# Moving one more destination block from the counted path to the gathered path in a two-layer graph network

## The chip, the core and the metric

The kernel runs on one core of a Trainium2 chip. The metric is device time in microseconds (us), the median over runs of the same program on the same inputs. The core has five engines with instruction queues of their own: PE (TensorE, matrix products, with its weight loads listed apart as PEld), DVE (VectorE), ACT (ScalarE), POOL (GpSimd) and SP (SyncE, which here only issues transfers). SBUF is the on-chip memory, PSUM holds the sums of PE.

## The reference, cut to what matters

There are 6250 nodes with 128 features, and 200,000 edges sorted by destination, each with a source node, a destination node and 128 features of its own. The destination is `6250 * u**2` of a uniform `u`, so low nodes have many edges and high nodes few.

```
h = relu(layernorm(x))
agg_src  = segment_sum(h[src], dst);  agg_edge = segment_sum(edge_attr, dst)
x = x + relu(concat(h, agg_src, agg_edge) @ W.T + b)
h = relu(layernorm(x))
twice:  h = relu(segment_sum(h[src], dst) / max(deg, 1) @ W_l + b + h @ W_r)
x = x + h
```

So three times a sum over edges of gathered rows is needed (called layers 0, 1 and 2 below), and once a sum of the edges' own features.

## The kernel before, in words

Nodes are cut into NB = 49 blocks of 128. Edges are cut into tiles of 128 and groups of 1024 (U = 8 tiles); there are 196 groups. The sum over edges of `h[src]` into one destination block can be had in two ways, and the kernel uses both.

**Counted blocks.** For the first NC = 40 destination blocks the kernel builds, once, a matrix of counts: how many edges go from each source node to each destination node. Then the sum over edges into a destination block is a matrix product of the counts with the rows of all 49 source blocks, and this is done anew in each of the three layers.

**Gathered (listed) blocks.** The last NT = 9 destination blocks have few edges. Their source rows are fetched in every layer by an indirect transfer, 128 rows at a time, and summed by a product with a one-hot matrix of destinations. `LISTS` gives, for each such block, its first edge tile and the tile after its last. Neighbouring blocks share the tile in which their border lies.

The program has two stages.

*Stage 1 (to about 590 us): counting and edge sums.* A loop over the stretches (runs of one to fourteen groups) and, in them, over the GC = 177 groups whose edges reach counted blocks. For a counted group DVE makes two one-hot matrices (`sp`, `sq`, line 533), weighs one of them (L543) and, for late groups, a correction `sc` (L533 again). PE multiplies them tile by tile (L740 and, for the correction, L751) into the PSUM tile `pu`, and ACT copies each tile's window into a ring in SBUF (L766). When a stretch is finished, POOL writes its ring to the DRAM matrix `counts_d` (L793). Between these products the sums of edge features are threaded in (`sum_edges`): for all 196 groups, counted or not, SP loads the edge features (L618), DVE makes a one-hot (L620), PE multiplies (L629) and DVE adds into `aggE` (L635). `shares` spreads these 1568 tiles evenly over the counted groups. The first layer's normalised rows are made in passing, one block in every third group (`first_layer`). The last group of the counted part has a stretch of its own with a narrower ring (`ENDS`, 152 and 82 columns for the last two stretches). After stretch `EARLY - 1` the counts of the first block are loaded ahead of time (L642, on POOL's queue).

*Stage 2 (from about 590 us): three layers of block sums.* `neighbours(i)` runs once for each of 3 x 40 = 120 pairs of layer and counted block. It has 49 dense products on PE (L929, one per source block), each 128x128 by 128x256 (the rows are split in a high and a low part). The counts come from DRAM in loads of 1088 KB (L642, SP), in bytes, and six "pieces" per block are widened to 32 bits by ACT or DVE (L861, and a short one at L864). After the block's sum come a reduction (L954), the layer's own arithmetic, a transpose (L475) and a product with the next layer's weights (L482), and the rows are written to `rows_d` and `r_d` (L488, L489).

Work for the gathered blocks is woven into the dense products at fixed places (`at_step`, an event before dense product `s`). Their tiles are cut into batches of at most three (BT = 3); before the change there are 149 tiles in 51 batches. `gather` issues one indirect transfer per tile on POOL (L1016) into one of ROWS = 4 buffers `rows_t`. `prepare` copies and splits the rows (L1033 on ACT, L1040 on DVE), makes the one-hot (L1034, DVE) and then asks for the gather four batches ahead. `sum_rows` has one product per tile and block (L1062, PE, 161 per layer). `prepare` stands LEAD = 38 dense products ahead of its `sum_rows`. The batches are spread evenly over the layer by

```python
begin = 4 * NB + NB // 2 if layer == 0 else 4 * NB
end = (NC - 2) * NB + 24 if layer < 2 else (NC - 1) * NB + 16
s = begin + (end - begin) * m // (len(batches) - 1)
```

which is one batch per 33 to 35 dense products. PE's order in stage 2 is tied by explicit dependencies ("in its turn among the dense products"); on ACT and DVE the same helpers tie the preparations behind what the dense products need, and a scheduler places the rest by its own estimate of times.

The kernel checks on the chip that its constants suit the edges (the tile ranges of `LISTS`, the windows, the ring widths); if they did not, a slow general version would compute everything again.

Of the kernel before, what the change touches and what calls it, by code (L numbers as in the profile page):

```python
# [32 lines left out]
NK = 2  # L33
NC3 = 3
PIECES = (("pair", 0, 4, 1), ("pair", 4, 8, 0), ("pair", 8, 12, 1), ("pair", 12, 17, 1), ("third", 0, 4, 0), ("third", 4, 8, 1))
GC = 177
GT = 176
LISTS = (
    (1414, 1433), (1432, 1451), (1449, 1468), (1466, 1484), (1483, 1501), (1499, 1518), (1517, 1535), (1533, 1550), (1549, 1563),
)  # L40
LATER = (1, 0, 0, 1, 0, 1)
FIRST = (1, 1, 1, 1, 0, 1)
# [39 lines left out]
ENDS = (152, 82)  # L82
# [4 lines left out]
def kernel(ctx: ExitStack, tc: tile.TileContext, x, srcl, dstl, edge, w0t, b0, w1l, b1, w1r, w2l, b2, w2r, out):  # L87
# [25 lines left out]
    NC = NB - NT  # L113
    NX = (G - GT) // 2
    assert 2 * NX == G - GT and U * NX <= P
    live_in_last = U - unused // P
    NE = sum(t1 - t0 for t0, t1 in LISTS)
    NL = (2 * NX - 1) * U + live_in_last
    assert LISTS[-1][1] == GT * U + NL and LISTS[0][0] >= GT * U
    CU = GC * U  # L120
    win_of = lambda g: REGIONS[min(g // RUN, NR - 1)][4]
    regions = []
    for i, reg in enumerate(REGIONS):
        if i * RUN < GC:
            regions.append((i * RUN, min((i + 1) * RUN, GC) if i + 1 < NR else GC) + reg)
    SWMAX = max(r[5] for r in regions)
    stretches = []
# [4 lines left out]
    place_of = lambda g: sum(U // n for n in size_of[:g])  # L132
    places = place_of(GC)
    g, ng, *reg = stretches.pop()
    stretches += [(g, ng - 1, *reg[:3], ENDS[0], reg[4]), (g + ng - 1, 1, *reg[:3], ENDS[1], reg[4])]
    NS = len(stretches)
    EARLY = NS - 6
    batches, tiles = [], list(range(LISTS[0][0], LISTS[-1][1]))
    while tiles:
# [6 lines left out]
        marks = sorted((j, u) for u, (_, m) in enumerate(batch) for j in m)  # L146
        batches.append((batch[0][0] - GT * U, len(batch), marks))
    assert sum(len(marks) for _, _, marks in batches) == NE
# [28 lines left out]

    fast = ExitStack()
    const = fast.enter_context(tc.tile_pool(name="const", bufs=1))
    small = fast.enter_context(tc.tile_pool(name="small", bufs=4))  # L180
    work = fast.enter_context(tc.tile_pool(name="work", bufs=2))
    keep = fast.enter_context(tc.tile_pool(name="keep", bufs=1))

# [21 lines left out]
    lists = build.enter_context(tc.tile_pool(name="lists", bufs=1))  # L205
    p_e = lists.tile([P, GC, U, 2], F16, name="p_e")
    q_e = lists.tile([P, GC, U, 2], F16, name="q_e")
    w_e = lists.tile([P, GC, U, 2], I16, name="w_e")
# [363 lines left out]
    def list_load(h, s):  # L572


        for k, a in enumerate((srcl, dstl)):
            at_s = bass.AP(
                tensor=a.tensor, offset=a.offset + P // U * s * GU + (GT + h * NX) * U, ap=[[U, NX], [GU, P // U], [1, U]]
            )
# [939 lines left out]
```

## Time and profile before

| | us |
|---|---|
| median of 9 runs | 1525.94 (1521.47 to 1533.72) |
| the profiled execution's own time | 1516.44 |
| its span, first to last instruction | 1514.8 |
| stage 1, first dense product starts at | 589.9 |
| stage 2, last dense product starts at | 1508.4 |

The profiled execution is 1.64 us longer than its span, and 9.5 us shorter than the median. In the profile's rows "busy" is the time in which at least one such instruction runs; matrix products overlap each other, so a row's mean duration is longer than the distance from one product to the next. The idle time in a row is that of its engine just before such an instruction, and the name behind the arrow is what ended it.

### The profile page before, as it was taken

The numbers are of one execution on the slowest core, as the hardware profiler recorded it, in microseconds if no ns is written. First come the engines' busy times: TensorE is split into PE (matmuls) and PEld (weight loads), VectorE is DVE, ScalarE is ACT, GpSimd is POOL, SyncE is SP. The second block draws the span as 40 slices with busy tenths as digits, with TensorE's granted clock in tenths as the row PEclk, the third lists the DMA queues.
The fourth block names the chain that finished last, engine by engine and source line by source line (L and its number), as shares of the span: only waits on it lengthen the run. The fifth ranks groups of instructions, "written<-read, shape, count | busy, mean of one in ns | idle before, by whom it ended". The sixth has DMA issues, their size and how long they took to land.

```text
span 1514.8 us, 37416 instructions
## 1 busy us (share of the span) xinstructions
PE 1422.1 (94%) x12433; PEld 1380.6 (91%) x12433; DVE 1161.8 (77%) x3007; ACT 924.4 (61%) x2251; POOL 684.0 (45%) x921
## 2 busy tenths in 40 slices
PE   5899999999999999999999997999899999999998
PEld 4899999998999998999899997999889998988997
DVE  9897989888898999677677775667766766666674
ACT  2434444567777778676666675666656675655563
POOL 4435576400000001666565604775666236666661
PEclk9999999999999999999999999999999998999999
DMA  2789888998999998877767765766666666776672
GB/s 72 236 275 288 281 302 307 327 314 309 315 317 339 343 358 313 275 234 230 228 209 233 233 215 194 247 227 199 201 200 213 209 220 194 242 222 212 219 249 76
DMA packets 173764, 374.02 MB, mean 247 GB/s; under 512 B 29451, under 2 KB 118985, under 8 KB 154234
## 3 DMA queue, kind: packets, MB, share of 16 engines
q1 hardware_dynamic: 121454, 268.72, 53.4%
q0 software_dynamic: 22336, 88.52, 17.3%
q10 hardware_dynamic: 29772, 14.31, 3.3%
q8 instruction: 100, 1.64, 0.4%
q14 instruction: 102, 0.84, 0.2%
HBM read 289.32 MB, written 82.13 MB: 245 GB/s over the span
## 4 chain that ended last, share of the span: by engine, by line
PE 70%; DVE 7%; issue 7%; ACT 6%; POOL 4%; DMA 3%; ACTq 1%; another core or an unknown queue 1%; SPq 0%; DVEq 0%; POOLq 0%
PE ps L929 36%; PE pe L629 20%; POOL rows_t L1016 4%; PE pu L740 4%; PE ps_t L1062 3%; ACT ring L766 3%; PE pz L482 3%; PE pu L482 1%; DMA rows_t<-rows_d,row_i 1%; ACT wide L861 1%; DMA x_c<-in_x 1%; PE pz L475 1%; ACTq L526 1%; DVE terms L877 1%
## 5 line engine op out<-in xcount | busy, mean ns | idle before, releaser
L929 PE MATMUL ps<-terms,wide 128*128 128x256 f32 (+1 forms) x5760 | 812.3, 292 | 14.4 <-issue 11.5
L929 PEld LDWEIGHTS ps<-terms,wide 128*128 128x128 f32 x5760 | 754.0, 199 | 24.0 <-issue 15.8
L1016 POOL DMA_INDIRECT rows_t<-rows_d,row_i x447 | 498.4, 1115 | 378.4 <-issue 112.6
L629 PE MATMUL pe<-hot,edge_t 128*128 128x128 f32 x3136 | 473.2, 287 | 2.9 <-DVE aggE L635 1.8
L629 PEld LDWEIGHTS pe<-hot,edge_t 128*128 128x128 f32 x3136 | 395.3, 192 | 6.5 <-DVE aggE L635 2.7
L861 ACT CAST wide<-c 128x1024 fp32r<-128x1024 uint8 x239 | 284.6, 1208 | 125.5 <-PE ps L929 76.8
L766 ACT CAST ring<-pu 128x170 f32 (+5 forms) x736 | 205.0, 281 | 85.2 <-PE pu L751 46.2
L861 DVE CAST wide<-c 128x1024 fp32r<-128x1024 uint8 x241 | 174.5, 727 | 104.3 <-PE ps L929 82.5
L861 ACT CAST wide<-c_early 128x1024 fp32r<-128x1024 uint8 x118 | 140.4, 1204 | 69.0 <-PE ps L929 53.2
L740 PE MATMUL pu<-sq,sp 128*128 128x102 bf16 (+7 forms) x1416 | 170.9, 219 | 9.7 <-DVE sq L543 4.3
L793 POOL DMA_DIRECT2D counts_d<-ring x50 | 27.2, 543 | 287.4 <-ACT ring L766 171.8
L773 POOL TENSOR_TENSOR ring<-ring,fore 128x17 int32 x280 | 112.8, 403 | 87.7 <-ACT fore L761 34.9
L740 PEld LDWEIGHTS <-sp 128*128 128x128 bf16 x1416 | 118.9, 98 | 12.3 <-issue 5.8
L861 DVE CAST wide<-c_early 128x1024 fp32r<-128x1024 uint8 x122 | 88.0, 722 | 53.7 <-PE ps L929 41.4
L533 DVE TENSOR_TENSOR sq<-iota,q_e 128x816 bf16<-128x816 f16 (+7 forms) x177 | 123.2, 696 | 4.7 <-PE pu L751 4.1
L533 DVE TENSOR_TENSOR sp<-iota,p_e 128x1024 bf16<-128x1024 f16 x177 | 121.8, 688 | 3.6 <-PE pu L740 2.7
L1040 DVE TENSOR_TENSOR tw<-rows_t,tw 128x384 fp32r<-128x384 f32 x153 | 83.2, 544 | 39.2 <-ACT tw L1033 35.7
L751 PE MATMUL pu<-sc,sp 128*128 128x17 bf16 x745 | 95.8, 172 | 0.0
L620 DVE TENSOR_TENSOR hot<-iota,rel 128x64 f32<-128x64 f16 (+13 forms) x196 | 94.6, 483 | 0.0
L1062 PE MATMUL ps_t<-tw,hot_t 128*128 128x256 f32 (+1 forms) x483 | 85.8, 286 | 3.5 <-issue 2.7
L1034 DVE TENSOR_TENSOR hot_t<-iota_p,slot_e 128x384 fp32r<-128x384 f16 (+1 forms) x153 | 87.2, 570 | 0.0
L482 PE MATMUL pz<-w_sb,hT 128*128 128x256 f32 x196 | 62.8, 403 | 25.8 <-ACT hT L477 18.3
(195 smaller groups left out, 1412.0 us busy)
## 6 DMA issues: line engine op xcount, KB each, us to landing
edge_t<-in_edge SPq DMA_DIRECT2D x196, 512.0 KB
c<-counts_d SPq DMA_DIRECT2D x80, 1088.0 KB
c_early<-counts_d SPq DMA_DIRECT2D x39, 1088.0 KB
rows_d<-feats ACTq DMA_DIRECT2D x147, 64.0 KB
r_d<-r SPq DMA_DIRECT2D x147, 64.0 KB
own<-r_d SPq DMA_DIRECT2D x147, 64.0 KB
counts_d<-ring POOLq DMA_DIRECT2D x5, 1462.0 KB
rows_t<-rows_d,row_i POOLq DMA_INDIRECT x447
```

The costliest lines, as they stand in the source:

```text
L482: mm = nc.tensor.matmul(pz, hT, w_sb[layer], start=True, stop=True)
L533: nc.vector.tensor_tensor(to.rearrange("p t (c two) -> p t c two", two=2), iota[:, :m].rearrange("p (c two) -> p c two", two=2).unsqueeze( ...
L620: nc.vector.tensor_tensor(hot[:, : U * win].rearrange("p (u w) -> p u w", w=win), iota[:, :win].unsqueeze(1).to_broadcast([P, U, win]), re ...
L629: mm = nc.tensor.matmul(ps[:, :P], e[:, u, :], hot[:, u * win : u * win + P], start=u == 0, stop=u == U - 1)
L740: mm = nc.tensor.matmul(pu[:, i * HALF : i * HALF + nq], sp[:, t, :], sq[:, t, :nq], start=t == t0, stop=t == t0 + n - 1 and n > 1,)
L751: mm = nc.tensor.matmul(pu[:, i * HALF : i * HALF + NJ], sp_b[:, t, :], sc[:, slot + 1 - len(last_tiles) + j0, :NJ], start=False, stop=j0 ...
L766: put = nc.scalar.copy(ring[:, bass.ds(to_put[(g - g0) * U + t0], nq)], pu[:, i * HALF : i * HALF + nq])
L773: add = nc.gpsimd.tensor_tensor(to, to, fore[:, i, :], op=ALU.add)
L861: copied = copy(t[:, : p1 - p0], two)
L929: dense = nc.tensor.matmul(ps[:, :m], counts, terms_of(s, s + 1)[:, 0, :m], start=s == 0, stop=s == NB - 1)
L1016: it = nc.gpsimd.indirect_dma_start(out=rows[:, u, :], out_offset=None, in_=rows_d[layer][:, :], in_offset=bass.IndirectOffsetOnAxis(ap=ro ...
L1062: mm = nc.tensor.matmul(ps[:, :width], hot[:, k, :], tw[:, u, :width], start=begins, stop=ends)
```

## The change

One more destination block, block 39, is taken from the counted path and put on the gathered one. NT goes from 9 to 10 and NC from 40 to 39. The counted groups end two earlier (GC 177 to 175), and the list of sources begins two groups earlier (GT 176 to 174). The new list covers tiles 1397 to 1414, 18 tiles, of which tile 1414 is shared with the next block. The last stretch of the counted groups now has one group only, so it is not split any more and the stretches are 50 instead of 51. One pool of small tiles has three buffers of each instead of four.

```diff
-GC = 177
-GT = 176
+GC = 175
+GT = 174
 LISTS = (
-    (1414, 1433), (1432, 1451), (1449, 1468), (1466, 1484), (1483, 1501), (1499, 1518), (1517, 1535), (1533, 1550), (1549, 1563),
+    (1397, 1415), (1414, 1433), (1432, 1451), (1449, 1468), (1466, 1484), (1483, 1501), (1499, 1518), (1517, 1535), (1533, 1550), (1549, 1563),
 )
...
     g, ng, *reg = stretches.pop()
-    stretches += [(g, ng - 1, *reg[:3], ENDS[0], reg[4]), (g + ng - 1, 1, *reg[:3], ENDS[1], reg[4])]
+    if ng > 1:
+        stretches.append((g, ng - 1, *reg[:3], ENDS[0], reg[4]))
+    stretches.append((g + ng - 1, 1, *reg[:3], ENDS[1], reg[4]))
...
-    small = fast.enter_context(tc.tile_pool(name="small", bufs=4))
+    small = fast.enter_context(tc.tile_pool(name="small", bufs=3))
```

Counted over the whole program, the instructions change as follows.

| engine | fewer | more |
|---|---|---|
| PE | 147 dense products (L929), 16 counts (L740), 16 corrections (L751) | 54 products of gathered rows (L1062) |
| DVE | 9 widenings (L861), 3 short ones (L864), 2 each of `sp`, `sq`, weighing and `sc` (L533, L543) | 18 one-hots (L1034), 18 splits (L1040) |
| ACT | 9 widenings (L861), 16 ring copies (L766) | 18 copies of gathered rows (L1033) |
| POOL | 1 write of a ring (L793) | 51 indirect transfers (L1016) |
| SP | 3 loads of counts (L642) | none |

The reductions, transposes and products with weights (L954, L475, L482) keep their number, since every block still passes through them, on one path or the other. The batches per layer go from 51 to 57, and the dense products from one batch to the next from 33.3, 33.8 and 34.6 (layers 0, 1, 2) to 28.9, 29.3 and 30.0.

## The prediction

> **What bounds the kernel now.** I read the page's busy lines and slices first, then the windows by stage, then the chain, then PE's own timeline for prices.
>
> ```profile
> PE   5899999999999999999999997999899999999998
> ...
> POOL 4435576400000001666565604775666236666661
> ```
>
> PE is at nine tenths or more nearly throughout. POOL is idle late in stage 1 and about 60% busy in stage 2. The windows say whether PE is waiting inside those slices:
>
> ```profile
> core 0: us, PE busy (x) PEld busy (x) DVE busy (x) ACT busy (x) POOL busy (x), PEclk, DMA share, GB/s
> 450.00:550.00 100.00, 99.65 (x1066) 97.37 (x1065) 90.61 (x196) 75.59 (x258) 5.84 (x11) 1.00 0.96 338
> 550.00:600.00 50.00, 45.16 (x444) 42.88 (x443) 46.30 (x87) 36.78 (x105) 3.20 (x6) 0.97 0.91 336
> ...
> 1300.00:1400.00 100.00, 92.59 (x727) 90.63 (x726) 64.72 (x143) 56.04 (x61) 64.68 (x57) 0.98 0.70 226
> 1400.00:1500.00 100.00, 96.00 (x765) 94.39 (x765) 68.10 (x154) 57.52 (x63) 54.92 (x51) 0.98 0.62 204
> ```
>
> Columns are busy us of PE, PEld, DVE, ACT and POOL. Stage 2 is PE's: 92.6 to 96 of 100 us, no other engine over 70. Late stage 1 is PE's too, with DVE close (90.6). At the end of stage 1 (550 to 590) the chain of waits runs through ACT's ring copies from 545 to 567 and from 583 to 588, and through PE between.
>
> So an edit is worth what it takes from PE, unless it makes something else late. The waits say how far POOL, which gets the new work, is from being late:
>
> ```profile
> POOL rows_t L1016 <- issue: 112.6, 355, 1.1
> POOL rows_t L1016 <- DVE tw L1040: 110.3, 47, 4.8
> ```
>
> 110.3 us in 47 waits POOL stood idle because the four buffers were full and `prepare` had not emptied one. It is ahead of its consumer. The 112.6 us in 355 waits are the 0.30 us between one gather and the next.
>
> **What the change removes and adds, in stage 2.** PE's stream in layer 2, from the chain of waits (start, us, what):
>
> ```profile
> 1486.73 4.24 PE ps L929 x35
> 1490.97 0.36 PE ps_t L1062 x3
> 1491.33 4.10 PE ps L929 x34
> 1495.43 0.35 PE ps_t L1062 x3
> ```
>
> A dense product costs 4.24/35 = 0.121 us, a product of gathered rows 0.36/3 = 0.12 us. (The page's 292 and 286 ns are overlapped durations and no prices.)
>
> - *Removed:* 3 layers x 49 dense products x 0.121 = 17.8 us. The block's reduction, transpose and weights stay, on the other path.
> - *Added:* 54 x 0.12 = 6.5 us.
> - *Net on PE:* -11.3 us. The other bound is the whole stage per block: (1508.4 - 589.9)/120 = 7.65 us, so -23.0 + 6.5 = -16.5 us. That holds if PE's stalls leave with the block. I take the first, since most stalls stand at transposes and weights (18.3 us of PE waiting for `hT`, ten times), whose number stays.
>
> *Beside PE.* ACT loses 9 widenings and gains 18 copies of gathered rows: -9 x 1.2 + 18 x 0.51 = -1.6 us. DVE loses 9 x 0.72 + 3 x 0.28 = 7.3 us and gains 18 x (0.57 + 0.54) = 20 us, over a stage where it is under 73% busy. Both stay beside PE. Where that cover is gone the whole 13 us of DVE would show; at that share I cost it at 0.7 us. SP issues three loads of 1088 KB less, POOL's queue 51 transfers of 128 rows more; transfers keep their engines 0.62 to 0.71 busy. I cost it at nothing.
>
> *POOL.* The gathers, by the page's group:
>
> ```profile
> L1016 POOL DMA_INDIRECT rows_t<-rows_d,row_i x447 | 498.4, 1115 | 378.4 <-issue 112.6
> ```
>
> 51 more at 1.115 + 0.30 = 1.415 us are 24 us per layer. Cover: a batch of 166/57 = 2.91 gathers takes 4.12 us. What does the layer give it? The preparations (L1033 on ACT) run from 622.8 to 891.5, 930.2 to 1206.5 and 1241.5 to 1497.7 us, 51 in each layer: one per 5.37, 5.53 and 5.12 us. After, each stretch loses 49 x 0.121 and gains 18 x 0.12, -3.8 us net, for 56 steps instead of 50: 4.73, 4.87 and 4.51 us. POOL's 4.12 fits in all three, at 87, 85 and 91%. The timeline also gives the distance from the end of a batch's last gather to its preparation: 4.2 and 4.5 us for the first batch of layers 1 and 2, at least 7.8 us elsewhere, mostly 12 to 18. Four batches ahead at 0.6 us less each cost some 2.5 us of that. So the gathers are hidden, though layer 2 keeps only a tenth in hand.
>
> *A rule against it.* The gather took 0.946 us at least, 1.026 us in the median and 2.967 us at most, beside a DVE that was two thirds busy. The Trainium skill, in "SBUF — State Buffer" (SBUF: two separate sides), says that a transfer issued from GpSimd can't write its descriptors while a two-port VectorE operation holds the shared port, and gives 620 ns alone against 3100 ns beside a copy. By that figure, as an estimate, 166 gathers of 3.1 + 0.3 us would take 564 us in a layer of some 300, and the change would be a heavy loss; the trace's mean of 1.115 us disagrees for this mix, and I go by it.
>
> **In stage 1.** PE's timeline late in the stage:
>
> ```profile
> 520.52 0.24 PE L740 MATMUL pu<-sq,sp 128*128 128x170 bf16 x1
> 520.59 0.17 PE L751 MATMUL pu<-sc,sp 128*128 128x17 bf16 x1
> 520.62 0.23 PE L740 MATMUL pu<-sq,sp 128*128 128x170 bf16 x1
> 520.69 0.17 PE L751 MATMUL pu<-sc,sp 128*128 128x17 bf16 x1
> 520.72 0.69 PE L629 MATMUL pe<-hot,edge_t 128*128 128x128 f32 x4
> ```
>
> Two tiles are counted in 520.72 - 520.52 = 0.20 us; a group has four such pairs, 0.8 us. The edge sums that follow stay, spread over 175 groups instead of 177. Two groups are 1.6 us of PE. By DVE a group costs 0.69 + 0.93 + 0.68 + 0.23 = 2.53 us (L533, L543 in the window 450 to 580), two 5.1; by ACT eight copies at 0.333 are 2.7, two 5.3. PE at 99.65 of 100 speaks for the first; the ACT-bound end for a part of the other. I take -2.2 us, between -1.6 and -5.3.
>
> The stretch that goes takes one write of POOL with it, where POOL is idle; nothing on the path. The early load of the first block's counts, which stands on POOL's queue behind the ring writes, moves from behind group 162 of 177 to behind 159 of 175, one group earlier seen from the end: nothing. The smaller setup (175 columns instead of 177 in 192 products, three more small DVE steps) is below 0.5 us either way. Three buffers instead of four: a block's `rstd` lives from 757.7 to 759.0 us in the one I looked at, and blocks come every 7 us, gathered ones between; so the third still covers. If it didn't, DVE would wait as it did for `rstd`, at most 2.6 us at a time.
>
> **Sum.** -11.3 - 2.2 + 0.7 = -12.8 us. The profiled execution's 1516.44 would become 1503.6 (span 1502.0). The median stands 9.5 us above that execution and should keep that distance: 1525.94 - 12.8 = **1513.1 us**. The measurement can tell about 0.3% from no change, that is 1521.4 to 1530.5.
>
> **Rivals.**
>
> - *More comes off than PE's bare pitch.* Stalls leave with the block (-16.5 us) and stage 1's end is ACT's (-5.3): -21.8 + 0.7, 1504.8 us. For it: the chain in ACT from 545 to 567. Against: PE at 99.65% just before, and stalls that belong to work that stays. Chance 0.18.
> - *The stalls are drawn anew.* Order on ACT and DVE is planned again, and PE had 54 us of gaps over 0.25 us from 580 us on, some of 3.6 to 7.5 us that the profile puts down to an unknown queue or to issue. A quarter more of them takes back 13 us: about 1526. For it: such gaps are not tied to a block. Against: nothing makes them more on average. Chance 0.15.
> - *POOL becomes the bound, slower than before.* Place: the interval of the gathers, layer 2 first. It decides from 4.51/2.91 - 0.30 = 1.25 us per gather; before it was 1.115. At 1.35 us a batch takes 4.80 us: 0.29 x 56 = 16 us in layer 2, 0.07 x 56 = 4 in layer 0, none in layer 1. Less the 12.8 gained, 1533 us. For it: the margin is a tenth, gathers up to 2.97 us exist, DVE gets busier. Against: 110 us of waits for buffers now, 12 to 18 us of lead. Chance 0.13.
> - *The change doesn't do what it says:* the checks on the chip find that a range doesn't fit, and the general version runs, at many times the time. The sorted destinations give node 4990 at the start of tile 1397 (it must lie below 4992) and 5120 at tile 1415 (at least 5120): it fits, narrowly. Chance under 0.01.
>
> The forecast itself, 1507 to 1520, gets 0.53. The range reaches to the first rival and to the second: 1502 to 1527. Faster by over 0.3%: 0.53 + 0.18 and 0.03 of the second, 0.74; within it 0.12; slower 0.14.
>
> **What would show it.** Right: the first dense product 1.6 to 5 us earlier than 589.9; from it to the last 11 us less than 918.5; the preparations 4.5 to 4.9 us apart; POOL's waits for `tw` well under 110 us but not gone. Wrong: waits of ACT's `tw` or PE's `ps_t` for `rows_t`, a mean gather above 1.25 us, or PE's gaps in stage 2 grown by more than 10 us.

## The result and the profile after

The changed kernel took **1572.67 us** (median of 20 runs, 1560.61 to 1587.39) against 1522.08 for the kernel before beside it; the ratio is 1.0343 with a 95% interval of 1.0323 to 1.0364. Ratios in this document leave out the few executions in a slower state, so they can differ by some thousandths from the quotient of the medians. The kernel is slower by 50.6 us, where 12.8 us less were forecast. The profiled execution took 1571.48 us, its span 1569.9, 55.1 more than before. In the profile after, line numbers are two higher: the dense products are L931, the gathers L1018, the copy of the transposed block `hT` L479, the product with weights L484.

First the page's slices, as they were shown of the kernel before:

```profile
PE   5899999899999998999888997989989999998898
...
POOL 4434567200000004656555605677666236776662
```

In stage 2 PE is no longer at nine tenths throughout: of its last 25 slices 22 read 9 before, and 15 do now. POOL's digits hardly move. The windows by stage:

```profile
core 0: us, PE busy (x) PEld busy (x) DVE busy (x) ACT busy (x) POOL busy (x), PEclk, DMA share, GB/s
450.00:550.00 100.00, 99.63 (x1060) 97.20 (x1059) 91.01 (x197) 74.91 (x258) 5.84 (x11) 1.00 0.94 336
...
1300.00:1400.00 100.00, 93.28 (x691) 89.81 (x689) 61.58 (x143) 52.45 (x58) 70.22 (x63) 0.93 0.64 209
1400.00:1500.00 100.00, 89.70 (x674) 85.84 (x674) 63.30 (x141) 53.09 (x58) 65.25 (x61) 0.97 0.67 215
```

Late stage 1 is as it was. In layer 2, 100 us hold 691 and 674 products instead of 727 and 765. DVE and ACT are less busy than before, not more: the engines wait for one another. What waits, over stage 2 (us in total, times, longest):

```profile
POOL rows_t L1018 <- issue: 128.2, 414, 1.0
...
POOL rows_t L1018 <- DVE tw L1042: 100.0, 42, 6.0
...
PEld ps L931 <- issue: 33.5, 62, 1.1
PE pz L484 <- ACT hT L479: 30.3, 23, 4.7
DVE wide L863 <- remote: 30.1, 10, 7.9
...
ACT wide L863 <- remote: 24.1, 10, 4.8
...
PE ps L931 <- issue: 22.7, 46, 1.1
```

POOL still waits for empty buffers (100.0 us in 42 waits, 110.3 in 47 before), so it is still ahead of its consumer. The group of the gathers says that a gather itself has not become slower:

```profile
L1018 POOL DMA_INDIRECT rows_t<-rows_d,row_i x498 | 551.6, 1108 | 377.3 <-issue 128.2
```

What grew stands on other engines. Before, the waits of the same four kinds were:

```profile
PE pz L482 <- ACT hT L477: 18.3, 10, 7.4
...
ACT wide L861 <- remote: 14.2, 5, 5.9
...
DVE wide L861 <- remote: 14.0, 7, 3.1
...
PE ps L929 <- issue: 11.5, 23, 0.9
```

PE's wait for `hT` at the product with weights went from 18.3 us in ten waits to 30.3 in 23; its waits for "issue", which are waits for nothing that the profile shows, from 11.5 to 22.7; ACT's and DVE's widenings waited 28.2 us for something "remote" before (14.2 + 14.0) and 54.2 now (24.1 + 30.1).

The account by stages, from the starts of PE's products. "Bare" is the number of products in stage 2 times 0.1215 us, the distance from one to the next where nothing disturbs them (4.24/35 before; `1477.31 3.61 PE ps L931 x30` in the chain after), and "rest" is what stage 2 lasts beyond that.

| us | before | after | |
|---|---|---|---|
| stage 1, to the first dense product | 589.9 | 593.4 | +3.5 |
| stage 2, first to last dense product | 918.5 | 970.4 | +51.9 |
| of it bare (6757 and 6664 products) | 821.0 | 809.7 | -11.3 |
| of it rest | 97.5 | 160.7 | +63.2 |
| of the rest, distances over 0.35 us too long | 64.9 (77 of them) | 114.0 (141) | +49 |

So PE has 93 products fewer, as forecast; the -11.3 us takes their pitch as unchanged, and the chain after shows it so (3.61/30 = 0.120). 63 us of something else stand against it. Part of them is PE's granted clock, which stood at half for 37.5 us of stage 2 before and for 71.7 after. A stretch at half clock can cost at most half its length, so by estimate this is at most 17 of the 63 us. Most of the rest are waits, and a stretch of the timeline after shows what they look like (start, us, engine, what, and in brackets the idle time before and what ended it):

```profile
969.26 0.30 ACT L980 ACTIVATE h<-y 128x128 f32<-128x128 f32 x1
...
969.62 0.33 PE L477 MATMUL pz<-ident,h 128*128 128x128 f32 x1 [2.89 <-ACT h L980]
...
969.70 1.46 PE L931 MATMUL ps<-terms,wide 128*128 128x256 f32 x8
970.58 0.95 POOL L1018 DMA_INDIRECT rows_t<-rows_d,row_i  x1 [0.31 <-issue]
...
974.72 0.55 DVE L1036 TENSOR_TENSOR hot_t<-iota_p,slot_e 128x384 fp32r<-128x384 f16 x1
...
975.58 0.27 ACT L479 COPY hT<-pz 128x128 f32<-128x128 f32 x1 [6.02 <-remote]
...
975.90 1.22 PE L484 MATMUL pz<-w_sb,hT 128*128 128x256 f32 x2 [4.74 <-ACT hT L479]
```

The copy of `hT` needs the transpose of 969.62 and nothing else, and ACT is free from 969.56 on; it starts at 975.58. DVE's one-hot at 974.72, which needs no product, runs meanwhile (behind a widening that itself waited 2.05 us), and POOL goes on gathering until 974.15.

The ends of products in a trace are modelled, but the trace also records when each semaphore, the counter by which engines tell one another that work is done, was incremented. PE started its last product before the stall at 970.75 and the next at 975.90. Five increments of PE's semaphore still came in between, at 974.08, 975.53, 975.56, 975.62 and 975.68, and ACT's copy started 0.02 us after the third. So ACT was not late to hear. The last three fit the transpose, for which ACT waited, and the fourth and eighth dense product behind it. They came 0.06 us apart, where four products take 0.49 us. That speaks for products that were done, and whose notice was held up.

Such late notices go with the gathers. In stage 1, which has no gathers, every recorded increment of PE came within 0.06 us of the modelled end of a product. In stage 2 of the kernel before, 60 of 1008 came over 1 us after the end of the last product that could have sent them, and 117 of 1056 after the change. Of those that came with no gather under way or in the 3 us before, 173 and 169, none was over 0.06 us late. The increments of ACT and DVE were never over 0.06 us late in these two profiles.

### The profile page after: what moved, and what is told of

The parts are those of the page before. It is cut to its first block, busy times and chain, and to the rows that moved or that the text cites. A ratio compares the mean times of both kernels' runs of the same rounds, so it can differ in the third digit from the quotient of the medians.

```text
span 1569.9 us, 37264 instructions
## 1 busy us (share of the span) xinstructions
PE 1440.4 (92%) x12308; PEld 1387.9 (88%) x12308; DVE 1166.1 (74%) x3024; ACT 915.9 (58%) x2244; POOL 734.3 (47%) x971
## 5 line engine op out<-in xcount | busy, mean ns | idle before, releaser
L931 PE MATMUL ps<-terms,wide 128*128 128x256 f32 (+1 forms) x5616 | 813.7, 295 | 26.9 <-issue 22.7
L931 PEld LDWEIGHTS ps<-terms,wide 128*128 128x128 f32 x5616 | 751.6, 202 | 42.6 <-issue 33.5
L1018 POOL DMA_INDIRECT rows_t<-rows_d,row_i x498 | 551.6, 1108 | 377.3 <-issue 128.2
L863 ACT CAST wide<-c 128x1024 fp32r<-128x1024 uint8 x233 | 277.8, 1206 | 163.7 <-PE ps L931 120.2
L863 DVE CAST wide<-c 128x1024 fp32r<-128x1024 uint8 x235 | 169.4, 725 | 121.4 <-PE ps L931 82.5
L768 ACT CAST ring<-pu 128x170 f32 (+5 forms) x720 | 200.2, 280 | 90.4 <-PE pu L753 54.2
L742 PE MATMUL pu<-sq,sp 128*128 128x170 bf16 (+7 forms) x1400 | 169.8, 220 | 10.5 <-DVE sq L545 3.9
L1042 DVE TENSOR_TENSOR tw<-rows_t,tw 128x384 fp32r<-128x384 f32 x171 | 92.7, 542 | 57.7 <-ACT tw L1035 49.8
L1036 DVE TENSOR_TENSOR hot_t<-iota_p,slot_e 128x384 fp32r<-128x384 f16 (+1 forms) x171 | 97.3, 569 | 10.1 <-PE ps L931 6.0
L1064 PE MATMUL ps_t<-tw,hot_t 128*128 128x256 f32 (+1 forms) x537 | 99.0, 293 | 2.9 <-issue 2.8
L484 PE MATMUL pz<-w_sb,hT 128*128 128x256 f32 x196 | 65.7, 418 | 36.1 <-ACT hT L479 30.3
```

Of the source, the lines that this page charges most:

```text
L484: mm = nc.tensor.matmul(pz, hT, w_sb[layer], start=True, stop=True)
L742: mm = nc.tensor.matmul(pu[:, i * HALF : i * HALF + nq], sp[:, t, :], sq[:, t, :nq], start=t == t0, stop=t == t0 + n - 1 and n > 1,)
L768: put = nc.scalar.copy(ring[:, bass.ds(to_put[(g - g0) * U + t0], nq)], pu[:, i * HALF : i * HALF + nq])
L863: copied = copy(t[:, : p1 - p0], two)
L931: dense = nc.tensor.matmul(ps[:, :m], counts, terms_of(s, s + 1)[:, 0, :m], start=s == 0, stop=s == NB - 1)
L1018: it = nc.gpsimd.indirect_dma_start(out=rows[:, u, :], out_offset=None, in_=rows_d[layer][:, :], in_offset=bass.IndirectOffsetOnAxis(ap=ro ...
```

## The experiments

The theory after this profile: the added gathers stall the other engines although they are done in time. Rivals: the smaller pool, the planner's new order of work, the transfers as such, and unbroken runs of gathers. All ratios are to the kernel before on the same chip.

### The small pool, and the number of gathers in both directions

Four kernels: the kernel before with three small buffers; the changed kernel with four (and one buffer for four tiles of the checks on the chip, to make room); the kernel before with 51 gathers more (17 tiles of each layer are gathered twice); the changed kernel with at most two gathers per batch, which leaves out the third tile of each (the rows buffers are fixed tiles, and DVE fills the third part with zeros once).

```diff
-    small = fast.enter_context(tc.tile_pool(name="small", bufs=4))
+    small = fast.enter_context(tc.tile_pool(name="small", bufs=3))
```

> The kernel before, with three buffers instead of four in the pool of small tiles, and nothing else. If the missing buffer is the cause (moments and rstd of the normalisation wait for the third tile back), it loses what layer 0 lost, 20 to 27 us: some 1545 us. If the cause is the gathers or the new order of the work, it stays at the 1522 us of before, within 5 us.

> The changed kernel with four buffers again in the pool of small tiles; room for them comes from four tiles of that pool that are used once (void, highest, again, again_i). If the missing buffer is the cause, layer 0 gets its 20 to 27 us back: some 1548 us. If not, it stays at 1573 us, within 6 us.

```diff
-        for u in range(n):
+        for u in [*range(n), *([0] if m % 3 == 1 else [])]:
```

> The kernel before, with 17 gathers more per layer: in every third batch the first tile's rows are fetched twice, into the same place. POOL and the transfers get the load of the change, the products, preparations and counts stay. If the gathers themselves are what slows the rest (their transfers, or POOL's writing of descriptors), it loses 30 us or more: 1550 us or above. If the order of the work or the preparations do it, it stays within 6 us of 1522.

```diff
-        for u in range(n):
+        for u in range(min(n, 2)):
```

> The changed kernel, whose batches gather only their first two tiles; the third part of each buffer stays zero and is summed as if it were rows (so the third tile's rows are left out of the sums). The preparations, products and counts stay as changed; POOL has a third less. If the gathers are the cause, it falls to the forecast of 1513 us or below. If the order or the preparations are the cause, it stays at 1565 us or above.

The pool is nothing: 1542.5 us, ratio 1.0001 (0.9966 to 1.0036), and 1602.13, 1.0372 (1.0333 to 1.0412). The kernel before with 51 gathers more, and neither block nor product changed, took 1619.89 us, **1.0474** (1.0407 to 1.0542). The changed kernel with 339 gathers instead of 498 took 1461.72 us, 0.9459 (0.9419 to 0.9499), and its rest in stage 2 is 37.8 us instead of 160.7. (Its first dense product came only at 608.7 us, though its last product of counts stood at 588.4, close to the 587.0 of before. Why isn't known; the ratio includes that loss.)

### Fewer gathered blocks

Eight and seven gathered blocks instead of nine (`GC`, `GT` and `LISTS` moved the other way; seven need one bound of a table changed).

```diff
-GC = 177
-GT = 176
+GC = 180
+GT = 178
 LISTS = (
-    (1414, 1433), (1432, 1451), (1449, 1468), (1466, 1484), (1483, 1501), (1499, 1518), (1517, 1535), (1533, 1550), (1549, 1563),
+    (1432, 1451), (1449, 1468), (1466, 1484), (1483, 1501), (1499, 1518), (1517, 1535), (1533, 1550), (1549, 1563),
```

> The change turned round: eight gathered blocks instead of nine (GC 180, GT 178, 41 counted blocks), 51 gathers fewer than before. By PE's bare pitch it must lose: 147 dense products more, 48 of the gathered kind fewer, three counted groups more, about +15 us against before, ratio 1.010. If each gather costs some 0.6 to 1 us of stalls in all engines, it wins 30 to 50 and loses 15: ratio 0.975 to 0.990.

> Seven gathered blocks (GC 182, GT 180, 42 counted blocks), 102 gathers fewer than before; the test of the windows counts its last region by (end - 1) // RUN, since 182 is a whole number of regions. By PE's pitch +28 us against before, ratio 1.018. If gathers cost 0.6 us each at this density, it wins 60 and loses 28: ratio 0.98. If the cost is steeper the denser the gathers are, it gains less over eight lists than eight lists gain over nine.

Eight took 1503.28 us, **0.9836** (0.9771 to 0.9901), and beat both kernels; seven took 1516.34, 0.9927 (0.9894 to 0.9961). With 393 and 342 gathers (54 and 105 fewer than before, where 51 and 102 were expected) the rest of stage 2 is 56.2 and 46.0 us. Stage 1 ends at 609.0 and 620.3, where it ended between 589.0 and 597.9 in the profiles that left it alone, and the last product of counts comes at 606.1 and 617.4 instead of 587.0. So counting these blocks cost far more there than the 0.8 us of PE per group.

### Is it the transfer, or its queue?

The kernel before with 51 plain loads of 64 KB into a rows buffer ahead of its gathers (which write over them), on POOL's queue and on SP's, and later 102 of them on POOL's, so that POOL is busy with them as long as with 51 gathers.

```diff
         rows = tail.tile([P, BT, D], F32, name="rows_t", bufs=ROWS)
+        if m % 3 == 1:
+            latest["POOL"] = nc.gpsimd.dma_start(rows[:, 0, :], rows_d[layer][P * (m // 3) : P * (m // 3 + 1), :])
```

On SP's queue it is `nc.sync.dma_start`; for 102 loads the condition is `if m % 3:`.

> The kernel before, with 17 plain transfers more per layer, issued by POOL: 128 consecutive rows of rows_d (64 KB) into the place that the first gather of the batch then overwrites. Same bytes and same queue as 51 gathers, but no index. If it is POOL's queue or its descriptors that hinder the others, it loses like the 51 gathers, ratio 1.03 to 1.05. If it is the indexed gather alone, it stays within 0.5% of before.

> The same 51 plain transfers of 64 KB, issued by SP instead of POOL. If the bytes or the transfer engines are what is short, it loses as the gathers do, ratio 1.03 or more. If it is POOL's issuing, it stays within 0.5% of before; SP may wait for the buffer, up to 5 us at a time, with the loads of counts behind it, which come four blocks ahead.

> The kernel before with 102 more plain transfers of 64 KB on POOL's queue (the gathers write over them), twice as many as in the run that cost nothing with 51, so that POOL is busy with them for as long as with 51 gathers (102 x 0.61 = 62 us against 51 x 1.09 = 56). If POOL's busy time or the number of its transfers is what counts, and 51 of the short ones were below a threshold: 1.03 to 1.06. If only indexed gathers cost: 0.998 to 1.012, 1518 to 1540 us.

51 on POOL: 1525.94 us, 1.0016 (0.997 to 1.0062). 51 on SP: 1532.98, 1.0063 (1.0028 to 1.0098), a loss of some 10 us. 102 on POOL: 1531.21, 0.9935 (0.9897 to 0.9973), no loss but a small gain that I can't explain. The groups of this last run (its gathers are at L1018, the copy of their rows at L1035):

```profile
L1018 POOL DMA_INDIRECT rows_t<-rows_d,row_i x447 | 507.7, 1136 | 298.4 <-issue 125.7
...
L1035 ACT CAST tw<-rows_t 128x384 fp32r<-128x384 f32 x153 | 77.2, 505 | 101.4 <-DMA rows_t<-rows_d,row_i 76.8
```

Here the rows are late, for once: ACT stood idle 76.8 us for gathers that had not landed, and POOL was busy 66 us more (102 x 0.647 in its own group). The time did not rise. So neither POOL's busy time, nor the bytes, nor rows that come late are what costs as the gathers do.

### Unbroken runs, scattered rows, and taking the gathers out again

In the traces PE's stalls cluster in long runs of gathers without a pause of 0.5 us: in the kernel before, PE was stalled for about 3% of the time or less at the second to sixth gather of a run, some 18% at the seventh to ninth and some 26% at the tenth to fifteenth. Does breaking the runs help? POOL fills the buffer ahead of every second batch.

```diff
         rows = tail.tile([P, BT, D], F32, name="rows_t", bufs=ROWS)
+        if m % 2 == 1:
+            latest["POOL"] = nc.gpsimd.memset(rows[:, :n, :], 0.0)
```

> The kernel before with a filling of the rows buffer by POOL ahead of every second batch's gathers, so that no more than six gathers follow one another without a pause of a us or so; the number of gathers (447) and all else stay. Theory R (TensorE, ScalarE and VectorE stall in long unbroken runs of gathers, from about the seventh on): the stretches of stall in stage 2, 65 us in the kernel before, fall to half or less, time 1480 to 1505 us. Theory N (it is the share of time in which POOL gathers, however it is cut): nothing is gained, and POOL is busier by the fillings, 1522 to 1545 us.

> Eight gathered blocks, 396 gathers, with the same fillings ahead of every second batch's gathers. Without them this version took 1503.3 us, 0.9836 of the kernel before. Theory R: its remaining stalls (30 us) mostly go, 1475 to 1495 us, 0.965 to 0.98. Theory N: 1500 to 1515 us, 0.98 to 0.99.

No run was longer than six, and the time was the same: 1516.78 us, 0.9979 (0.9935 to 1.0022). The rest of stage 2 was 88.0 us, against 97.5 in the profile of before. With eight blocks (393 gathers by the trace) it was 1500.2, 0.9889 (0.9798 to 0.998), no better than without. My theory of the runs falls: they are where stalls show, not what a gather costs.

The same kernel as with 51 gathers more, but with consecutive rows; and 51 more that take 32 rows each.

```diff
+    nc.gpsimd.iota(straight, pattern=[[0, 1]], base=0, channel_multiplier=1)
...
-        for u in range(n):
+        for at, u in enumerate([*range(n), *([0] if m % 3 == 1 else [])]):
...
-                in_offset=bass.IndirectOffsetOnAxis(ap=row_i[:, t + u : t + u + 1], axis=0),
+                in_offset=bass.IndirectOffsetOnAxis(ap=row_i[:, t + u : t + u + 1] if at < n else straight, axis=0),
```

And for the short ones:

```diff
-                out=rows[:, u, :],
+                out=rows[:32, u, :] if few else rows[:, u, :],
...
-                in_offset=bass.IndirectOffsetOnAxis(ap=row_i[:, t + u : t + u + 1], axis=0),
+                in_offset=bass.IndirectOffsetOnAxis(ap=row_i[: 32 if few else P, t + u : t + u + 1], axis=0),
```

> The kernel before with 51 more gathers as in the run that added them (+72 us), but these take rows 0 to 127 in turn and not scattered ones (they write over one tile's rows, so the gathered sums are not the reference's). If scattered addresses in memory cost the time: most of it is gone, 1526 to 1550 us. If it is the indexed instruction and what POOL does for it: 1590 to 1625 us as with scattered rows.

> The kernel before with 51 more gathers as in the run that added them (1.0474), but each of these takes 32 rows and not 128 (the rows of a tile's first 32 edges once more). If the price is one of the instruction itself: 1.04 to 1.06, 1580 to 1605 us. If it goes by the rows that a gather describes and moves: a quarter of the 72 to 88 us, 1.01 to 1.02, 1532 to 1550 us.

Consecutive rows: 1600.12 us, **1.0579** (1.0487 to 1.0671). 32 rows: 1619.24, **1.0517** (1.0429 to 1.0604). Neither the addresses nor the number of rows made a difference that these runs can tell. The first of these two against the run with 51 plain loads on POOL is the sharpest pair of the study: 128 consecutive rows of 512 bytes both times, from one engine's queue into one buffer, and 88 us against nothing. The queue that carries the gathers held the same packets and bytes in both, first with the 51 gathers, then with the 51 loads:

```profile
q0 software_dynamic: 23968, 91.86, 16.6%
```

```profile
q0 software_dynamic: 23968, 91.86, 17.7%
```

The two groups of the gathers on POOL, those of the kernel before and the 51:

```profile
L1018 POOL DMA_INDIRECT rows_t<-rows_d,row_i x447 | 487.0, 1089 | 352.6 <-issue 115.3 <-DVE tw L1042 84.4 <-DMA xt<-x_d 46.8
...
L1018 POOL DMA_INDIRECT rows_t<-rows_d,straight x51 | 55.5, 1087 | 48.8 <-DMA rows_t<-rows_d,row_i 35.4 <-issue 13.2 <-DVE rstd L464 0.3
```

Last, the changed kernel and the kernel before with 51 gathers fewer (the rows buffers are fixed tiles, and 17 batches of each layer gather two tiles of three; in the kernel before, batches 5 and 8 are among them).

```diff
-        rows = tail.tile([P, BT, D], F32, name="rows_t", bufs=ROWS)
-        for u in range(n):
+        rows = rows_of[m % ROWS]
+        for u in range(2 if m % 3 == 1 and m >= ROWS else n):
```

> The changed kernel, in which 17 of the batches of each layer gather two tiles instead of three (the third keeps older rows, so the sums of the gathered blocks are not the reference's); products, copies, one-hots and blocks are those of the changed kernel, the gathers are as many as before, 447. If the added gathers cost the time (theories N and R alike): the time comes back to the forecast, 1505 to 1525 us, stage 2 from 970 to some 915 us. If the planner's new order of work on ScalarE and VectorE, or the 56 batch steps, cost it (rival D): 1555 to 1575 us.

> The kernel before with 396 gathers instead of 447 (17 batches of each layer gather two tiles of three; the third keeps older rows, so the sums of the gathered blocks are not the reference's). If every gather costs the same 1.4 to 1.7 us: 72 to 88 us less, 1435 to 1450 us. If the price rises with POOL's share of the layer: most of the 65 us of stalls in stage 2 go, but no more, 0.965 to 0.985, 1465 to 1500 us. If 447 gathers still fit for nothing and only those above cost: 0.995 to 1.0.

The changed kernel came back to 1515.05 us, **1.0000** (0.9968 to 1.0031): its whole loss against the kernel before goes with the 51 gathers. It keeps the planner's new order, the 56 steps and all other work of the change, so these can't be what made it slower. They may still have cost up to the 12.8 us that the change was to bring and that don't show. (The fixed tiles weren't tried by themselves.) The kernel before with 396 gathers took 1489.44, **0.967** (0.9626 to 0.9713).

### What a gather costs

| gathers | rest of stage 2, us | kernels |
|---|---|---|
| 339, 342 | 38, 46 | changed with two of three; seven blocks |
| 393 to 396 | 54 to 66 | eight blocks, with and without fillings; before with 51 fewer |
| 447 | 88 to 124 | before (97.5), with fillings, with three small buffers, with plain loads; changed with 51 fewer |
| 498 | 161 to 206 | changed (160.7), with four small buffers; before with 51 more of three kinds |

The number of gathers orders every profile, whatever else differs. In time, with the kernel before of the same chip as the base: 51 fewer give 0.033 x 1540.43/51 = 1.0 us per gather; the last 51 of the changed kernel cost 0.0343 x 1522.08/51 = 1.0; 51 more in the kernel before cost 0.0474 x 1543.57/51 = 1.4 to 0.0579 x 1518.02/51 = 1.7. From seven blocks to eight the rest grew by only 10.2 us for 51 gathers, 0.2 each, in one profile each. So the price of one more rises with the number there are. The share of the time in which POOL gathers doesn't order the last row: it is 57% of stage 2 in the changed kernel and 53% with 51 more in the kernel before, and the second lost more. There each added gather writes where another has just written and waits for it, which may be why; that was not tried.

The late notices follow the same order: over 1 us late were 5 and 12 of PE's increments with 339 and 342 gathers, 22 to 33 with 393 to 396, 31 to 77 with 447 (31 with 102 plain loads beside them) and 106 to 157 with 498, of 980 to 1056 in each profile.

## Why the prediction was wrong, point by point

- *The change does what it says:* right. 498 gathers, 147 dense products fewer, the bare pitch of stage 2 down by 11.3 us as forecast (-17.8 + 6.5).
- *Stage 1, -2.2 us:* +3.5 in the profile. Profiles of kernels with an unchanged stage 1 end it anywhere from 589.0 to 597.9 us, so two groups fewer can't be told there either way. That more groups do lengthen the stage is shown by the eight and seven blocks: 609.0 and 620.3.
- *"So the gathers are hidden":* **this is the step that failed**, with "SP issues three loads of 1088 KB less, POOL's queue 51 transfers of 128 rows more; [...] I cost it at nothing". The cover itself was judged rightly: the mean gather was 1.108 us (limit 1.25), POOL still waited 100.0 us for buffers, and a batch's last gather ended at least 6.2 us ahead of its preparation (4.8 for the first batch of layer 1), 11.8 to 14.5 in the medians of the layers. But being in time is not being free. Each added gather cost the stage 1.0 to 1.7 us: 51 x 1.0 = 51 us by the run without them. By the traces, what comes with the gathers is that the notices of PE's products are late, so that ACT and DVE wait for them, and then PE for ACT and DVE.
- *POOL becomes the bound, 1533 us, from 1.25 us per gather:* the mechanism did not occur, though the sign did. The run with 102 plain loads had rows 76.8 us late at no cost.
- *The stalls are drawn anew, 1526 us:* the right symptom, priced at a quarter and argued away with "nothing makes them more on average". The distances over 0.35 us went from 64.9 to 114.0 us, by three quarters, and the number of gathers makes them more. The new order itself is not the loss (1.0000 with 51 fewer), though it may hide in the next point.
- *More comes off than the bare pitch:* no sign of it. With 51 fewer the changed kernel should have stood at 0.9916 (1513.1/1525.94), and stood at 1.0000. In its profile 11.3 us left the bare pitch and the rest was 112.6 us instead of 97.5, which is inside the 88 to 124 of kernels with 447 gathers. Where those 13 us went is open, and so is the 0.7 us put down for DVE, a term that no run shows.
- *Three small buffers:* covered, as said (1.0001).
- *The signs that were named:* the preparations came 5.21, 5.15 and 4.68 us apart and not 4.73, 4.87 and 4.51; PE's gaps grew by 49 us, where over 10 was to mean wrong. The waits for `rows_t` and the mean gather, named as the other two, stayed in order: I had looked for harm only where the gathers' own result is used.
- *The rule on the shared port:* the Trainium skill, "SBUF — State Buffer" (SBUF: two separate sides), would have made gathers slower beside VectorE. That is not what happened; the mean gather went from 1.115 to 1.108 us. Nor did DVE's operations on two inputs get longer beside more gathers: the split took 0.544 us before and 0.542 after, the one-hot 0.570 and 0.569. Whether any of them is a two-port operation, no run shows.

What could have been seen: the trace of before held 97.5 us of stage 2 beyond the bare pitch, and stalls in which ACT waited up to 8.1 us for a "remote" release after a transpose, while POOL gathered. I took those as belonging to "work that stays", and did not ask which engine was active in them. Nor are "most stalls" the 18.3 us at `hT`: the distances over 0.35 us were 64.9 us too long in all.

## What to carry to other kernels

An operation that is done in time on an idle engine can still cost the engine that bounds; costing it at nothing needs a run with more of it, not only a slack. When a profile has stalls with no releaser ("remote", "issue"), list what the other engines do during them, and double and halve the suspect alone. Here an indexed gather of up to 128 rows was worth about 1 us of the whole kernel at 450 gathers in 920 us, so a block with 3 x 17 gathers of its own costs some 51 us and 6.5 of products on the gathered path. On the counted path it costs 17.9 us of products and, by the kernel with eight gathered blocks, by estimate some 17 us of stage 1 (609.0 against 592, the mean of the unchanged ones). Of the four splits that ran, seven to ten gathered blocks, the best was one gathered block less, not one more.

## What the runs showed of the hardware

- Indirect transfers issued by POOL made PE, ACT and DVE wait, and plain ones of the same 128 x 512 bytes from the same queue did not: 1.0579 against 1.0016 for 51. The Trainium skill, in "DMA: Bandwidth & Descriptors" (SWDGE vs HWDGE vs iDMA), treats DMAs issued from GpSimd alike, direct and indirect; these runs tell them apart.
- 32 rows instead of 128 cost the same (1.0517 against 1.0474).
- While POOL gathers, the semaphore increments of PE's products come late, by up to 7.9 us in the kernel before, counted from the last product that could have sent them, and those of ACT and DVE don't. More than 3 us after a gather none of PE's is late in the profiles before and after. What in the chip holds them up is open. It was not tried by itself.
- PE's mean granted clock fell with the stalls, from 0.985 to 0.970 in the profiles; with 51 gathers more in the kernel before it was 0.955, where that chip gave the kernel before 0.972 to 0.982. That the stalls lower the clock, and not the clock the pace, was not tried.
